# Two transformer layers on one core: query feature products moved to GpSimd, an elu without tanh, one more dense sequence, and a fixed priority table

## The chip, the cores and the metric

The kernel runs on one core of a Trainium2 chip, as one launch. Its time is device microseconds for the whole launch; a run's number is the median over executions. All tensors are float32.

## The reference, cut to what matters

The input is `x` of 8 sequences with 512 tokens of 128 features. Four blocks follow one another, each with a residual sum and a layer normalization.

```python
def feats(data, proj, is_query):               # random features, per head (16 heads of 64)
    dash = einsum('bnhd,md->bnhm', data * dn, proj)          # 64 features
    diag = sum(data**2, -1, keepdims=True) * dn*dn / 2
    mx = max(dash, -1) if is_query else max(dash)
    return ratio * (exp(dash - diag - mx) + 1e-6)

# block 1: linear attention, its own FFN and norms
qf, kf = feats(x@Wq, proj, True), feats(x@Wk, proj, False)
num = qf @ (kf^T v);  den = qf . sum_n(kf)                   # per head
out1 = layernorm(x + (num / den) @ Wo, g1, b1)
x = layernorm(x + layernorm(out1 + elu(out1@W1 + b1) @ W2 + b2, g2, b2'))
# block 2: mixture of 8 experts of width 64, top 2, every expert computed
x = layernorm(x + sum_e gates[e] * (gelu(x@w1[e] + b1[e]) @ w2[e] + b2[e]))
# block 3: softmax attention, 16 heads of 8, rotary
x = layernorm(x + softmax(rot(q) rot(k)^T / sqrt(8)) v @ wo + bo)
# block 4: mixture of 8 experts of width 176, top 2, and a shared expert
h = silu((x@w1[e] + b1[e]) * (x@w3[e] + b3[e]))
x = layernorm(x + sum_{2 chosen e} score[e] * (h@w2[e] + b2[e]) + shared(x))
```

## The kernel before, in words

**Stages.** `keys()` runs first, over all 8 sequences: key features, their exponentials, per sequence a 128 x 1024 product `xes`, and the sums of the key features over tokens, `z8` (8 x 1024, one row for each sequence, stored to `z_d`). It ends with a product `kvo` per sequence, stored to `kvo_d`. Then a loop runs over the sequences b. `linear_attention_and_ffn` (block 1) works in four tiles of 128 tokens. Its inner `features(t)` makes the query features: two projections into PSUM (L898, L908), Square on ScalarE (L903), sum (L905) and maximum (L914) per head, subtraction (L918), Exp (L919), the product with the row `zr` of key sums (L922), the sum of it per head (`den`, L924), its reciprocal (L926) and the scaling (L927). `attend(t)` transposes them (L937), copies (L941) and multiplies with `kvo` (L945). `features(t + 1)` is recorded ahead of `attend(t)`. The feed-forward has four chunks of 128 hidden units on 512 tokens (L970 to L979), with elu as Relu + min((Exp + 1) * Tanh, 0). `first_mixture` is block 2. `softmax_attention` (block 3) has 16 steps: four matmuls for 4 heads (L1147), Exp over 128 x 2048 in two activations (L1153), four matmuls with the values (L1159).

**Block 4 has two forms.** `GROUPS` lists the sequences that are sorted: `sort` scatters a sequence's tokens twice each with 8 indirect DMAs on GpSimd into `x_d` (L1469), by expert, and computes the shared expert (L1557, L1566). When a group is complete, `tiles` fetches weights and 256 tokens for each of a list of tiles, with `most = 2*N*n // TR + E2 - 1` entries for n sequences (L1620, L1626, L1634), and `combine` gathers the results of each sequence with 8 indirect DMAs (L1477) and sums them with the gates (L1653). A sequence in no group goes through `dense_mixture`: all experts and the shared one, as 13 chunks of 128 hidden units (L1328, L1329 the two projections, L1331 to L1339 the gating, L1353 the second product). Its weights `fw1`, `fw3`, `fw2` are loaded by `side_by_side`, after the linear attention of sequence 7 is recorded, and lie over the places of that stage.

**Places.** One SBUF tile `scratch` is cut by hand. On one side, from `feed_forward_at` on, lie the rings `f_zr`, `f_kvo`, `f_hT`, `f_res`, `f_o1`, `f_t0`, `f_t1`, then `a_xT`, `a_rot_q` and others. `fw1`, `fw3`, `fw2` (1664 elements each) and `m_gr` (5 x 512) lie from `feed_forward_at` on as well:

```python
fw1, fw3, fw2 = (scratch[:, feed_forward_at + FC2 * P * n :][:, 0 : FC2 * P] for n in range(3))
("m_gr", feed_forward_at + 3 * FC2 * P, 5), ("m_ta", KEYS_SCRATCH, 4), ("m_tb", KEYS_SCRATCH + 4 * N, 4),
```

**Order.** Every operation is first recorded in a `Schedule`, with an estimated time and with its dependences by place: two operations on overlapping places, one of which writes, keep the order in which they were recorded. `order()` then puts them in line: `latest_alone` gives each a latest start (from the due times, 40 us a sequence), and `forward` simulates all engines and takes next the operation that can start first, and among equals the one with the smaller latest start. It also chooses PSUM banks. Each operation belongs to a part, (stage, sequence): 0 linear attention, 1 first mixture, 2 softmax attention, 3 sort or dense mixture, 4 tiles, 5 combine, 6 `side_by_side`, and None. Before the change 400 rounds of random shifts of these parts follow, and the order with the shortest simulated span is issued. Each engine executes its own instructions in that order.

Of the kernel before, what the change touches and what calls it, by code (L numbers as in the profile page):

```python
# [30 lines left out]
F32 = mybir.dt.float32  # L31
AF = mybir.ActivationFunctionType
ALU = mybir.AluOpType
# [3 lines left out]
P = 128  # L37
# [14 lines left out]

GROUPS = ((0, 1, 2, 3), (4, 5, 6))

# [22 lines left out]
WAITS = mybir.DependencyInfo(mybir.DependencyClass.Sync, mybir.DependencyReason.DATA)  # L77
ROUNDS = 400
LATER = 8
PERIOD = 40.0  # L80


# [16 lines left out]
class Schedule:  # L99
# [171 lines left out]
    def order(self):  # L271

        self.tilings = [
            (self.tiling(w.calls[0]), self.tiling(w.calls[-1])) if w.engine == "PE" else None for w in self.works
        ]
        urgency = self.latest_alone()  # L280
        best = self.forward(urgency)
        again = self.backward(*best[:2])
        better = self.forward(again)
        if better is not None and better[0] < best[0]:
            best, urgency = better, again
        parts = sorted({w.part for w in self.works}, key=str)
        shift, chance = dict.fromkeys(parts, 0.0), random.Random(1)
        for _ in range(ROUNDS):
            trial = dict(shift)
            for _ in range(chance.choice((1, 1, 2, 3))):  # L290
                trial[chance.choice(parts)] += chance.gauss(0.0, chance.choice((3.0, 10.0, 30.0)))
            found = self.forward([u + trial[w.part] for u, w in zip(urgency, self.works)])
            if found is not None and found[0] <= best[0]:
                best, shift = found, trial
        self.makespan, self.starts, self.bank = best
        return [i for _, i in self.starts]

    def latest_alone(self):

        works, line, open_ = self.works, [], [len(w.before) for w in self.works]  # L300
        ready = [i for i, n in enumerate(open_) if not n]
        while ready:
            line.append(ready.pop())
            for j in works[line[-1]].after:
                open_[j] -= 1
                if not open_[j]:
                    ready.append(j)
        assert len(line) == len(works)
        latest = [0.0] * len(works)
        for i in reversed(line):  # L310
            w, end = works[i], self.ends[i]
            for j in w.after:
                end = min(end, latest[j] - self.HANDOVER[w.engine])
            latest[i] = end - max(w.us, w.lands)
        return latest

    def backward(self, span, starts):

        works, free = self.works, dict.fromkeys(self.HANDOVER, 0.0)
        key, latest, at = [0.0] * len(works), [0.0] * len(works), [0.0] * len(works)  # L320
        for start, i in starts:
            key[i] = -(start + works[i].us)
        open_, ready = [len(w.after) for w in works], {e: [] for e in free}
        for i, w in enumerate(works):
            if not w.after:
                bisect.insort(ready[w.engine], (key[i], i))
        for _ in works:
            best = None
            for e, waiting in ready.items():
                for entry in waiting:  # L330
                    end = max(free[e], at[entry[1]])
                    if best is None or end < best[0]:
                        best = (end, e, entry)
                    if end <= free[e]:
                        break
            end, e, entry = best
            ready[e].remove(entry)
            i = entry[1]
            free[e] = end + works[i].us
            done = end + max(works[i].us, works[i].lands)  # L340
            latest[i] = span - done
            for j in works[i].before:
                f = works[j].engine
                at[j] = max(at[j], done + (self.HANDOVER[f] if f != e else self.KEPT[f]))
                open_[j] -= 1
                if not open_[j]:
                    bisect.insort(ready[f], (key[j], j))
        return latest
# [121 lines left out]
def kernel(ctx: ExitStack, tc: tile.TileContext, i: dict, out: bass.AP):  # L470
# [104 lines left out]

    hb1 = keep("hb1", [P, FC])
    nc.vector.tensor_scalar(hb1, cols[:, C_B1 : C_B1 + FC], 0.5, None, ALU.mult)
    gb1 = keep("gb1", [P, 2])
# [5 lines left out]
    b1, fb = (rows[:, at : at + D] for at in (R_B1, R_FB2))  # L584
    nc.vector.tensor_tensor(b1, b1, fb, ALU.add)
    vv = keep("vv", [P, NT, V1])
    nc.gpsimd.memset(vv, 1.0)


    kvo_d = tc.dram_tile([B, P, 8, D], F32, name="kvo_d")  # L590
    z_d = tc.dram_tile([B, HM], F32, name="z_d")
    g1_d = tc.dram_tile([B, E1, N], F32, name="g1_d")
# [29 lines left out]
    def keys():  # L622
# [147 lines left out]
        )  # L770
        nc.sync.dma_start(z_d, z8)

# [39 lines left out]
    feed_forward_at = top["r"]  # L812
    ring("f_zr", 1, HM)
    ring("f_kvo", 1, 8, D)
    ring("f_hT", 1, FC, N)
    for name, n in (
        ("f_res", 2), ("f_o1", 1), ("f_t0", 2), ("f_t1", 2),
        ("a_xT", 1), ("a_rot_q", 1), ("a_rot_k", 1), ("a_t", 3), ("e_t", 2), ("a_o1", 1), ("a_res", 1), ("a_xa", 2),
        ("m_res", 1), ("m_xs", 1), ("m_ya", 2), ("m_t0", 1),
    ):  # L820
        ring(name, n, N)
# [64 lines left out]
    def linear_attention_and_ffn(b, xT):  # L886
# [7 lines left out]
        def features(t):  # L894
# [26 lines left out]
            pr = tile2("f_sp")  # L921
            nc.vector.scalar_tensor_tensor(pr, eq, EPS_KERN, zr, ALU.add, ALU.mult)  # L922
            den = tiny("f", [P, H], "den")
            nc.vector.tensor_reduce(den, hm(pr), AX.X, ALU.add)  # L924
            rden = tiny("f", [P, H], "rden")
            nc.vector.reciprocal(rden, den)  # L926
# [41 lines left out]
        for c in range(FC):  # L968
# [6 lines left out]
            nc.scalar.activation(ex, hp, AF.Exp, bias=bias)  # L975
            th = tile2("f_t1")
            nc.scalar.activation(th, hp, AF.Tanh, bias=hb1[:, c : c + 1], scale=0.5)
            nc.vector.scalar_tensor_tensor(ex, ex, 1.0, th, ALU.add, ALU.mult)
            nc.vector.scalar_tensor_tensor(hT[:, c, :], ex, 0.0, hT[:, c, :], ALU.min, ALU.add)  # L979
        fp = psb("fp", "f")  # L980
# [324 lines left out]
    def dense_mixture(xb, dst):  # L1305
# [15 lines left out]
        def hidden(c):  # L1321
# [15 lines left out]
            if gated:  # L1337
                nc.gpsimd.tensor_tensor(up, up, gr, ALU.mult)
            nc.vector.scalar_tensor_tensor(gr, ua, 1.0, up, ALU.add, ALU.mult)  # L1339
# [177 lines left out]
    def sort(b, xa, begin, group, rows_d):  # L1517
# [25 lines left out]
        for t in range(NT):  # L1543
            for k in range(2):
                nc.do(
                    "gpsimd", scatter(group), (rows_d,), (xa[:, t, :], slots[:, b, k, t : t + 1]),
                    1.05, 3.3, ("slots", group),
                )
# [95 lines left out]
    def combine(b, group, rows_d, dst):  # L1644
# [3 lines left out]
        for k in range(2):  # L1648
            y = tok(tile2("m_ya"))
            for t in range(NT):  # L1650
                nc.do("gpsimd", gather(group), (y[:, t, :],), (rows_d, slots[:, b, k, t : t + 1]), 1.05, 3.3)
            for t in range(NT):
# [155 lines left out]
```

## Time and profile before

| | |
|---|---|
| time, median of 3 runs | 1266.55 us (1265.4 to 1269.11) |
| the profiled execution: time, span | 1267.01 us, 1264.9 us |
| TensorE (PE) busy | 1152.9 us, 91% |
| VectorE (DVE) busy | 874.3 us, 69% |
| ScalarE (ACT) busy | 716.5 us, 57% |
| GpSimd (POOL) busy | 376.5 us, 30% |
| mean granted clock of TensorE | 0.954 |

Busy times overlap: the engines work side by side, and each waits for others by semaphores. A group's line reads: line of the kernel, engine, operation, destination <- sources, shape, count | busy us in all, mean ns of one | idle time of the engine just before them, and what ended it. `scratch` is the hand-cut tile, `ps` is PSUM. PEld is the weight load of TensorE. Matrix products in float32 take two passes, so each matmul of the code is two instructions in the profile. Sequences follow one another at some 115 us; the stages of neighbouring sequences overlap.

### The profile page before, as it was taken

How to read it: one execution, taken by the hardware profiler on the slowest of the kernel's cores; microseconds unless marked ns; L12 is line 12 of the kernel's file. 1: busy time of each engine (PE TensorE's matmuls, PEld its weight loads, DVE VectorE, ACT ScalarE, POOL GpSimd, SP SyncE). 2: the span in 40 equal slices, each digit the busy share in tenths (PEclk: the TensorE clock that was granted, in tenths of full speed). 3: DMA queues.
4: the chain of work that ended last, by engine and by line, in shares of the span. 5: the costliest groups of instructions: out<-in, count | busy, mean ns of one | idle time of the engine just before them, and what ended most of it. 6: DMA issues, size and time to landing. Idle time of an engine off the chain costs nothing. (4 is left out here: it accounts for less than half of the span.)

```text
span 1264.9 us, 17709 instructions
## 1 busy us (share of the span) xinstructions
PE 1152.9 (91%) x6262; PEld 626.0 (49%) x6262; DVE 874.3 (69%) x1940; ACT 716.5 (57%) x964; POOL 376.5 (30%) x375
## 2 busy tenths in 40 slices
PE   8999999978899999999899989999999885899972
PEld 4444445645543445535444546465456333654641
DVE  6766664988953964876885895678639477654763
ACT  3443444546377657576676555856664774277531
POOL 1242240022402400700720273122002877400174
PEclk9999999989999989999999989999999996899985
DMA  7038902301011002001101104223321224443241
GB/s 213 3 94 269 312 1 85 113 18 67 10 51 34 1 9 76 25 26 42 43 1 42 47 26 154 90 79 94 113 64 47 85 71 123 144 134 104 73 131 52
DMA packets 86747, 100.14 MB, mean 79 GB/s; under 512 B 17640, under 2 KB 62755, under 8 KB 86653
## 3 DMA queue, kind: packets, MB, share of 16 engines
q1 hardware_dynamic: 82765, 91.04, 23.6%
q0 software_dynamic: 3584, 7.35, 1.9%
q8 instruction: 51, 0.84, 0.3%
q10 hardware_dynamic: 304, 0.56, 0.1%
q14 instruction: 43, 0.35, 0.1%
HBM read 62.01 MB, written 39.93 MB: 81 GB/s over the span
## 5 line engine op out<-in xcount | busy, mean ns | idle before, releaser
L1153 ACT ACTIVATE scratch<-ps 128x1024 f32<-128x1024 f32 x256 | 248.9, 1022 | 103.8 <-PE ps L1147 102.8
L1147 PE MATMUL ps<-scratch 32*128 32x512 f32 x1024 | 163.4, 666 | 16.3 <-ACT scratch L1153 6.6
L1159 PE MATMUL ps<-scratch,vv 128*32 128x512 f32 x1024 | 140.7, 618 | 0.5 <-ACT scratch L1153 0.5
L853 POOL TENSOR_TENSOR f_ln_rs<-f_ln_ve,nhalf 128x4 f32<-128x4 f32 x24 | 27.5, 1146 | 212.1 <-DVE f_ln_ve L851 205.8
L664 ACT ACTIVATE scratch<-ps 128x1024 f32<-128x1024 f32 x32 | 32.7, 1023 | 92.4 <-PE ps L659 92.4
L1147 PEld LDWEIGHTS ps<-scratch 32*128 32x128 f32 x1024 | 45.7, 189 | 73.1 <-issue 22.4
L945 PEld LDWEIGHTS ps<-scratch 128*128 128x128 f32 x512 | 60.4, 192 | 19.1 <-issue 11.7
L1477 POOL DMA_INDIRECT scratch<-x_d,slots x56 | 56.3, 1005 | 41.6 <-DMA x_d<-scratch 24.0
L1626 PE MATMUL ps<-scratch 128*128 128x256 f32 x252 | 65.3, 398 | 1.6 <-DMA scratch<-w_d 0.8
L945 PE MATMUL ps<-scratch 128*128 128x128 f32 x512 | 64.0, 278 | 2.9 <-DVE a_ss L1013 1.0
L1123 POOL TENSOR_TENSOR scratch<-x_sb,rows 128x512 f32<-128x512 f32 x8 | 10.9, 1363 | 186.9 <-PE ps L613 184.5
L1469 POOL DMA_INDIRECT x_d<-scratch,slots x56 | 60.7, 1084 | 18.9 <-issue 14.7
L898 PE MATMUL ps<-wq,scratch 128*128 128x512 f32 x128 | 63.5, 603 | 0.8 <-DVE scratch L1094 0.8
L675 DVE SCALAR_TENSOR_TENSOR scratch<-k_ssq,ps 128x1024 f32<-128x1024 f32 x32 | 38.9, 1215 | 36.3 <-PE ps L669 32.4
L908 PE MATMUL ps<-wqf,scratch 128*128 128x512 f32 x128 | 63.4, 608 | 0.4 <-DVE scratch L1172 0.4
L1159 PEld LDWEIGHTS ps<-scratch,vv 128*32 128x32 f32 x1024 | 20.6, 109 | 82.0 <-issue 60.9
L659 PE MATMUL ps<-scratch 128*128 128x512 f32 x128 | 60.0, 608 | 0.7 <-ACT scratch L652 0.7
L698 PE MATMUL ps<-scratch,x_sb 128*128 128x512 f32 x128 | 59.4, 597 | 0.0
L669 PE MATMUL ps<-scratch 128*128 128x512 f32 x128 | 58.8, 598 | 0.0
L919 ACT ACTIVATE scratch<-scratch 128x1024 f32<-128x1024 f32 x32 | 33.9, 1058 | 43.1 <-DVE scratch L918 43.0
L1626 PEld LDWEIGHTS ps<-scratch 128*128 128x128 f32 x252 | 46.2, 195 | 20.1 <-issue 5.9
L941 ACT COPY scratch<-ps 128x1024 f32<-128x1024 f32 x32 | 32.3, 1010 | 34.3 <-PE ps L937 34.1
(281 smaller groups left out, 2528.7 us busy)
## 6 DMA issues: line engine op xcount, KB each, us to landing
x_d<-scratch SPq DMA_DIRECT2D x32, 512.0 KB, 8.5
scratch<-w_d SPq DMA_DIRECT2D x42, 386.0 KB, 3.1
scratch<-g_d SPq DMA_DIRECT2D x66, 128.0 KB, 3.1
scratch<-x_d SPq DMA_DIRECT2D x42, 128.0 KB, 2.1
x_d<-scratch SPq DMA_DIRECT2D x42, 128.0 KB, 1.9
kvo_d<-scratch SPq DMA_DIRECT2D x8, 512.0 KB, 5.7
scratch<-z_d SPq DMA_DIRECT2D x8, 512.0 KB, 4.4
scratch<-kvo_d SPq DMA_DIRECT2D x8, 512.0 KB
```

Source lines behind the costliest of these rows:

```text
L659: nc.tensor.matmul(kp_ps[:, a, :], xT[:, t * P : (t + 1) * P], wk[:, a * 512 : (a + 1) * 512], start=True, stop=True,)
L669: nc.tensor.matmul(dp_ps[:, a, :], xT[:, t * P : (t + 1) * P], wkf[:, a * 512 : (a + 1) * 512], start=True, stop=True,)
L698: nc.tensor.matmul(xp_ps[:, a, :], x_of(b)[:, t, :], ek[:, t, a * 512 : (a + 1) * 512], start=(t == 0), stop=(t == NT - 1),)
L898: nc.tensor.matmul(qp[:, a, :], xT[:, t * P : (t + 1) * P], wq[:, a * 512 : (a + 1) * 512], start=True, stop=True,)
L908: nc.tensor.matmul(dp[:, a, :], xT[:, t * P : (t + 1) * P], wqf[:, a * 512 : (a + 1) * 512], start=True, stop=True,)
L945: nc.tensor.matmul(at_ps[:, 0:D], qnT[:, c, :], kvo[:, c, :], start=(c == 0), stop=(c == 7))
L1147: nc.tensor.matmul(halves[g // 2][:, g % 2, :], kr[quarter, kt * P : (kt + 1) * P], qz[quarter, j, :], start=True, stop=True, tile_positio ...
L1153: nc.scalar.activation(pr[:, 2 * a : 2 * a + 2], sc, AF.Exp)
L1159: nc.tensor.matmul(av[32 * g : 32 * g + 32, :], vv[:, kt, head_columns(4 * g + j)], pr[:, g, :], start=(kt == 0), stop=(kt == NT - 1), til ...
L1469: inst = tc.nc.gpsimd.indirect_dma_start(out=rows_d, out_offset=bass.IndirectOffsetOnAxis(ap=slots_, axis=0), in_=tokens_, in_offset=None)
L1477: inst = tc.nc.gpsimd.indirect_dma_start(out=to, out_offset=None, in_=rows_d, in_offset=bass.IndirectOffsetOnAxis(ap=slots_, axis=0))
L1626: nc.tensor.matmul(to, w[:, c : c + P], xf, start=True, stop=True)
```

## The change

Four things are changed. (1) In `features`, the product of the query features with `zr` is a plain multiplication on GpSimd; the 1e-6 that was added to the features ahead of it becomes one number per head, made once per sequence in `keys()` (`z8e`), carried in 16 further columns of `z_d` and added to `den`. (2) elu is Relu + min(Exp, 1) - 1, and the -1 is taken out of the bias `b1` as the column sums of W2 (`less`); the Tanh, its bias `hb1`, one VectorE operation a chunk and the ring `f_t1` go. (3) `GROUPS` has sequences 0 to 3 and 4, 5; sequences 6 and 7 are both dense; the multiplication with the gates in the dense chunks goes from GpSimd to VectorE. (4) The planner starts from a fixed table of shifts by part and runs no rounds; the backward pass is gone, and its estimates for scatter and gather are 1.31 and 1.25 us instead of 1.05.

```diff
-GROUPS = ((0, 1, 2, 3), (4, 5, 6))
+GROUPS = ((0, 1, 2, 3), (4, 5))
...
-ROUNDS = 400
+ROUNDS = 0
+URGENT = {
+    (0, 0): 0.1, (0, 1): 12.6, (0, 2): -1, (0, 3): 35.5, (0, 4): 15.3, (0, 5): -2.6, (0, 6): 0.6,
...
+    (2, 4): -24.8, (2, 5): 25.4, (2, 6): -709.5, (2, 7): -55.9, (3, 0): 31.9, (3, 1): -290.8, (3, 2): 0.5,
+    (3, 3): -68.7, (3, 4): 183.1, (3, 5): 0.6, (3, 6): 81.4, (3, 7): 216.3, (4, 0): -18.1, (4, 1): 76.6,
+    (5, 0): 434, (5, 1): 631.3, (5, 2): 417.2, (5, 3): 926.4, (5, 4): 479.3, (5, 5): 341.1, (6, 0): -508.3,
+    None: 3.6,
+}
...
         urgency = self.latest_alone()
-        best = self.forward(urgency)
-        again = self.backward(*best[:2])
-        better = self.forward(again)
-        if better is not None and better[0] < best[0]:
-            best, urgency = better, again
...
+        shift, chance = {p: URGENT.get(p, 0.0) for p in parts}, random.Random(1)
+        best = self.forward([u + shift[w.part] for u, w in zip(urgency, self.works)])
...
+    less = nc.banks(1, 0)[:, 0, 0:D]
+    with nc.together():
+        for c in range(FC):
+            nc.tensor.matmul(less, ones, w2[:, c, :], start=(c == 0), stop=(c == FC - 1))
+    nc.vector.tensor_tensor(b1, b1, less, ALU.subtract)
...
-    z_d = tc.dram_tile([B, HM], F32, name="z_d")
+    z_d = tc.dram_tile([B, HM + H], F32, name="z_d")
...
-        nc.sync.dma_start(z_d, z8)
+        z8e = tiny("k", [B, H], "z8e", 1)
+        nc.vector.tensor_reduce(z8e, z8.rearrange("p (h m) -> p h m", m=M), AX.X, ALU.add)
+        nc.vector.tensor_scalar(z8e, z8e, EPS_KERN, None, ALU.mult)
+        nc.sync.dma_start(z_d[:, 0:HM], z8)
+        nc.sync.dma_start(z_d[:, HM:], z8e)
...
-    ring("f_zr", 1, HM)
+    ring("f_zr", 1, HM + H)
...
-        ("f_res", 2), ("f_o1", 1), ("f_t0", 2), ("f_t1", 2),
+        ("f_res", 2), ("f_o1", 1), ("f_t0", 2),
...
-            nc.vector.scalar_tensor_tensor(pr, eq, EPS_KERN, zr, ALU.add, ALU.mult)
+            nc.gpsimd.tensor_tensor(pr, eq, zr[:, 0:HM], ALU.mult)
             den = tiny("f", [P, H], "den")
             nc.vector.tensor_reduce(den, hm(pr), AX.X, ALU.add)
+            nc.vector.tensor_tensor(den, den, zr[:, HM:], ALU.add)
...
-            th = tile2("f_t1")
-            nc.scalar.activation(th, hp, AF.Tanh, bias=hb1[:, c : c + 1], scale=0.5)
-            nc.vector.scalar_tensor_tensor(ex, ex, 1.0, th, ALU.add, ALU.mult)
-            nc.vector.scalar_tensor_tensor(hT[:, c, :], ex, 0.0, hT[:, c, :], ALU.min, ALU.add)
+            nc.vector.scalar_tensor_tensor(hT[:, c, :], ex, 1.0, hT[:, c, :], ALU.min, ALU.add)
...
             if gated:
-                nc.gpsimd.tensor_tensor(up, up, gr, ALU.mult)
+                nc.vector.tensor_tensor(up, up, gr, ALU.mult)
...
                     "gpsimd", scatter(group), (rows_d,), (xa[:, t, :], slots[:, b, k, t : t + 1]),
-                    1.05, 3.3, ("slots", group),
+                    1.31, 3.6, ("slots", group),
...
-                nc.do("gpsimd", gather(group), (y[:, t, :],), (rows_d, slots[:, b, k, t : t + 1]), 1.05, 3.3)
+                nc.do("gpsimd", gather(group), (y[:, t, :],), (rows_d, slots[:, b, k, t : t + 1]), 1.25, 3.6)
```

## The prediction, made before the result was known

> **What bounds the kernel now.** The page's first table says TensorE, its windows say where not.
>
> ```profile
> PE 1152.9 (91%) x6262; PEld 626.0 (49%) x6262; DVE 874.3 (69%) x1940; ACT 716.5 (57%) x964; POOL 376.5 (30%) x375
> ```
>
> The span of 1264.9 us is 1152.9 of TensorE work and 112.0 of TensorE idleness, so a forecast is one for each of the two. The profiled execution took 1267.0 us, 2.1 outside its span; the median of the runs is 1266.55, so a span plus 1.7 stands for the median. Next the windows of 32 us: columns are the stretch, its length, busy time (and count) of PE, PEld, DVE, ACT and POOL, granted clock, DMA share, GB/s.
>
> ```profile
> 256.00:288.00 32.00, 22.41 (x95) 14.55 (x94) 27.46 (x61) 15.32 (x23) 7.85 (x6) 0.89 0.06 18
> 320.00:352.00 32.00, 28.10 (x139) 17.13 (x137) 31.43 (x73) 11.57 (x18) 13.27 (x12) 0.90 0.02 9
> 384.00:416.00 32.00, 31.14 (x192) 13.00 (x189) 13.39 (x32) 25.65 (x37) 7.59 (x7) 1.00 0.11 34
> 608.00:640.00 32.00, 28.28 (x142) 15.18 (x140) 29.58 (x47) 19.30 (x30) 22.11 (x24) 0.95 0.05 15
> 1056.00:1088.00 32.00, 16.95 (x70) 11.89 (x68) 18.68 (x82) 7.99 (x15) 20.62 (x34) 0.68 0.40 129
> 1216.00:1248.00 32.00, 21.32 (x103) 15.68 (x101) 16.89 (x42) 10.64 (x20) 23.76 (x23) 0.82 0.39 107
> ```
>
> TensorE idles where VectorE is nearly full (27 to 31 of 32 us) and hardly where VectorE is at 13. Adding up 32 minus the PE column over all windows: 6 us idle before 224, 18 in 224 to 352 (the first query features, nothing else to run yet), 36 in 352 to 1056, 15 in 1056 to 1088, 3 up to 1184, 34 from there to the end. The same windows have a granted clock of 0.68 to 0.95; busy time multiplied by one minus the clock gives some 24 us of stretched TensorE work in 224 to 1056, 5 in 1056 to 1088, 8 in the tail. The groups by line tell what fills VectorE there:
>
> ```profile
> L922 DVE SCALAR_TENSOR_TENSOR scratch<-scratch 128x1024 f32<-128x1024 f32 x32 | 38.9, 1216 | 7.5 <-ACT scratch L919 7.3
> L978 DVE SCALAR_TENSOR_TENSOR scratch<-scratch 128x512 f32<-128x512 f32 x32 | 22.9, 728 | 10.2 <-ACT scratch L977 10.1
> L977 ACT ACTIVATE scratch<-ps,hb 128x512 f32<-128x512 f32 x32 | 22.3, 697 | 0.0
> L708 POOL TENSOR_TENSOR scratch<-scratch 128x1024 f32<-128x1024 f32 x8 | 18.8, 2356 | 2.7 <-ACT scratch L693 2.7
> ```
>
> One token tile of query features costs VectorE L905, L914, L918, L922, L924, L927 at about 1.21 each and small ones, 8.2 us in all, against 7.1 of TensorE (L898, L908, L937, L945: 228.2 us over 32). Last the end: one line of TensorE's timeline, then the chain of waits (start, us, what):
>
> ```profile
> 1173.28 1.06 PE L1159 MATMUL ps<-scratch,vv 128*32 128x512 f32 x8
> ...
> 1195.11 1.05 POOL scratch L1477
> ...
> 1218.56 1.27 POOL scratch L1338
> ...
> 1248.97 1.07 POOL scratch L1477
> 1250.05 1.07 POOL m_ln_rs L853
> ```
>
> Attention of sequence 7 ends with these L1159, at 1174.3. The 91 us after it run on GpSimd: 24 gathers of the three sorted sequences, 1.25 apart, mixed with the 11 gate multiplications (L1338) of the dense sequence, whose L1353 matmuls wait for them (11.4 us in PEld's waits).
>
> **The change, part by part.** *Multiplication with the key sums to GpSimd.* VectorE loses 32 x 1.216 = 38.9 us and gains 32 small additions (den + zr's tail), 0.17 to 0.33 each by L916, the nearest 128x16 row: 5 to 10, I take 6. GpSimd gains 32 x 2.36 = 75.5 (L707 to L709, same shape); with 376 busy before it has room. The chain of one tile grows by 2.36 - 1.22 and one more handover (0.1 to 0.2 between neighbours in the timeline), 1.3 us; features(t+1) runs ahead of attend(t) and covers it; uncovered it is 32 x 1.3 = 42 us. VectorE's sum of a tile (L924) now waits for GpSimd, and L926, L927 and whatever VectorE has queued wait behind it. The long holders of GpSimd's queue there are the 8 scatters of a sorted sequence (1.27 to 1.39 us apart in the timeline), one instruction each, so one costs the multiplication at most 1.3 us of delay. z_d's second part costs one reduction and one tiny operation once, about 1.4 us of VectorE at 220, and one more DMA on SP: 1 us.
>
> *elu.* 32 Tanh activations (22.3 us of ScalarE) and 32 L978 (22.9 of VectorE) go; L979 stays in its form. The four `less` matmuls, once, in the setup: 0.5 us of TensorE.
>
> *Sequence 6 dense instead of sorted.* TensorE gains 13 chunks: 52 passes of 512 columns at 0.483 (L1557: 20.3/42) and 104 passes of 128 at 0.148 (L1566: 16.6/112), 25.1 + 15.4 = 40.5 (46.0 as the one dense sequence ran, at clock 0.82). It loses the shared expert (L1557, L1566: 2.9 + 2.4), the counting (0.8) and, since the list of group 1 shrinks from 19 tiles to 15, four tiles of 3.07 (L1620 16.8, L1626 65.3, L1634 46.8 over 42): 18.4. Net +22. GpSimd loses 8 scatters and 8 gathers (21 us with their gaps) and 11 L1338 (13.8), VectorE gains 22 multiplications of 0.74 (L1063's mean, 16.3) and about 20 of dense work, and loses 21 of sorting, tiles and combining. On SP four times two fetches and a store go, with sequence 6's store and load of xs_d; its gate rows and store of g2_d come.
>
> *The order.* All instructions are placed anew by a planner whose priorities are now a fixed table. Its worth has no row; I bound it by the idle time it can shift, the 36 + 15 + 3 us between 352 and 1184: none gained, or 30.
>
> **The sum, by stretches.** VectorE sheds 38.9 + 22.9 - 6 = 56 us, all in query features and feed-forward, where it is full. In 224 to 352 (8 tiles of 32, so 14 us) I let TensorE gain 10 of the 18 idle; in 352 to 1056 the other 42, cut by 10 for the lock below to 32, of which half, 18, reaches TensorE, because it idles in a part of these windows only. With less idle time I take a third of the stretched 24, 8 us, back. 1056 to 1088: the idle time came from sequence 6's routing ahead of tiles (L1526 waited 6.5 for L1522); dense work in its place leaves 8 of 15, and 3 of clock. Tail: attention output, normalization and router, 11.7 us from these operations' means and 0.1 a handover; 13 chunks at 2.9 with a fill of 4: 42; last sum and normalization 6.5; from there to the span's end 8.3, as now (1256.6 to 1264.9). Together 68.5 instead of 90.6, with 40 us of TensorE in it: 29 idle, 3 of clock won back. Idle: 7 + 8 + 18 + 8 + 5 + 29 = 75. Busy: 1152.9 + 22.5 - 8 - 3 - 3 = 1161.4. Span 1236.4, with 1.7 outside **1238**.
>
> **A rule against it.** GpSimd and VectorE get in each other's way in this trace:
>
> ```profile
> 521.98 1.26 POOL L1096 TENSOR_TENSOR scratch<-scratch 128x512 f32<-128x512 f32 x1
> 522.03 1.23 DVE L860 SCALAR_TENSOR_TENSOR a_ln_nm<-a_ln_mv,a_ln_rs 128x4 f32<-128x4 f32 x1 [1.58 <-POOL a_ln_rs L853]
> L916 DVE SCALAR_TENSOR_TENSOR f_nb<-f_ssq,f_mxq x32: 127/168/1239, 217.9 to 977.4; 128x16 f32<-128x16 f32 x32
> ```
>
> A VectorE operation of 0.16 us took 1.23 and ended with GpSimd's. L916 (minimum, median, maximum in ns) reaches 1239, L927 2108 over a median of 1215. Mean minus median, summed over L916, L927, L860, L979, L1285 and L1537, is some 21 us now. The multiplication adds 75.5 us of GpSimd beside 56 us of relief. By the rows' rate (21 us in 376 of GpSimd) it costs VectorE 4 us; if every one stops a VectorE operation for half its length, 32 x 1.18 = 38. I took 10. [...]
>
> **Rivals.** *All relief arrives* (0.23): idle time in 224 to 1056 falls from 54 to 14 and half the stretched 24 returns: 1238 - 12 - 4, and a few more in 1056 to 1184: **1219**. For it: VectorE is the only engine near full there. Against: the first features have nothing beside them, whichever engine is shorter.
>
> *The lock eats the relief* (0.08): 38 us of 56, and GpSimd's own waits the rest; 224 to 1056 keeps its idle time and clock, 1238 + 10 + 18 + 8 = **1274**. It decides once each multiplication meets one of its neighbours L916, den or L927. Against: they are three short turns of some 8 us.
>
> *Dense sequence 6 stands in attention 7's way* (0.13), the slower side: dropping f_t1 moves a_xT and a_rot_q down by 1008 elements; the dense part's ring m_gr (5 x 512 behind three 1664-wide weights, ending at 7552), now reaches past 6672 into both. Attention 7 cannot write its transposed input until the tenth chunk of sequence 6 is done. If nothing covers that, the front of dense 6 (11.7 + 4), the rest of its chunks' gaps (8) and attention 7's projections (8) stand open: 1238 + 32 = **1270**. It decides if group 1's 15 tiles (46 us of TensorE) and sequence 7's first mixture are used up before. For it: 1056 to 1088 now. Against: both become ready at that time.
>
> *The new order brings nothing* (0.04): table and costs fit no better, gains and the extra 22 us cancel: **1266**.
>
> **The numbers.** The forecast has 0.52, by itself 1226 to 1252. A measurement of this kernel tells about 0.3%, 4 us, from no change. Faster: 0.52 + 0.23 + 0.03 of the third rival: 0.78; same 0.05; slower 0.17. The range, 1214 to 1272, holds forecast, full relief and most of the third rival.
>
> **What would show it.** Right: L922 gone from DVE, a POOL line of 2.36 us x32, VectorE near 840 us, PE 1155 to 1175, windows with VectorE at 25 or less in query features and PE above 30 there, the end 65 to 72 us behind the last L1159 (90.6 now) without gathers in the chain. Wrong: PE idle 100 us or more; the chain waiting on GpSimd in query features; a stretch without L1147 while dense 6 runs with idle TensorE.

## The result, and the profile after

| | before | after |
|---|---|---|
| time, median of 4 runs each, taken side by side | 1265.97 us | 1225.57 us (1222.53 to 1226.43) |
| ratio, with its 95% interval | | 0.9673 [0.9648, 0.9699] |
| the profiled execution: time, span | 1267.01, 1264.9 us | 1222.53, 1220.7 us |
| TensorE idle, of the span | 112.0 us | 80.5 us |
| mean granted clock | 0.954 | 0.981 |
| time with the clock at half, added up from the trace's clock records | 119.6 us | 47.7 us |

The change makes the kernel 40 us faster; 28 were forecast. From the page after, the row of busy times and the row of granted clock in 40 slices; under them the clock row of the page before:

```profile
PE 1140.2 (93%) x6340; PEld 623.6 (51%) x6340; DVE 871.3 (71%) x1916; ACT 706.1 (58%) x943; POOL 417.5 (34%) x370
...
PEclk9999999989999999999999999999999999999988
```

```profile
PEclk9999999989999989999999989999999996899985
```

TensorE has 78 instructions more than before and is busy 12.7 us *less*. VectorE, which was to be relieved to some 840 us, is at 871, where it was. These two numbers are what the rest of this document is about. Four of the windows of 32 us that are shown of the kernel before (busy time and count of PE, PEld, DVE, ACT, POOL, then granted clock, DMA share, GB/s):

```profile
256.00:288.00 32.00, 27.11 (x121) 18.01 (x119) 23.16 (x49) 15.21 (x21) 14.27 (x8) 0.89 0.09 30
320.00:352.00 32.00, 27.99 (x151) 18.91 (x149) 28.87 (x66) 15.61 (x25) 19.83 (x14) 0.92 0.02 9
608.00:640.00 32.00, 29.88 (x146) 14.05 (x145) 31.56 (x45) 24.61 (x34) 21.62 (x14) 1.00 0.06 19
1056.00:1088.00 32.00, 29.90 (x180) 24.26 (x179) 25.20 (x54) 12.81 (x24) 1.01 (x1) 0.95 0.60 172
```

1056 to 1088 is filled: 29.9 of TensorE instead of 17.0. At 608 VectorE is as full as it was (31.6 us). The first query features (256, 320) still leave 4 to 5 us of each window idle, although 14 to 20 us of GpSimd now stand there. The groups of the changed lines, each shape by itself (busy, mean ns | idle time before and what ended it):

```profile
L912 POOL TENSOR_TENSOR scratch<-scratch 128x1024 f32<-128x1024 f32 x32 | 78.0, 2437 | 121.0 <-ACT scratch L909 74.7 <-ACT scratch L779 30.4 <-DVE f_den L914 12.5
L918 DVE SCALAR_TENSOR_TENSOR scratch<-scratch,f_rden 128x1024 f32<-128x1024 f32 x32 | 43.6, 1362 | 1.0
L914 DVE TENSOR_REDUCE f_den<-scratch 128x16 f32<-128x1024 f32 x32 | 38.6, 1205 | 11.3 <-POOL scratch L912 11.3
L967 DVE SCALAR_TENSOR_TENSOR scratch<-scratch 128x512 f32<-128x512 f32 x32 | 31.6, 999 | 4.8 <-ACT scratch L966 4.8
L915 DVE TENSOR_TENSOR f_den<-f_den,scratch 128x16 f32<-128x16 f32 x32 | 11.9, 372 | 0.2
```

L912 is the product on GpSimd, L914 the sum that waits for it, L915 the small addition, L967 the one operation left of elu's two on VectorE. L967 "stays in its form", as the prediction has it of L979, and its mean still went from 738 ns to 999; L979 before:

```profile
L979 DVE SCALAR_TENSOR_TENSOR scratch<-scratch 128x512 f32<-128x512 f32 x32 | 22.9, 738 | 2.9 <-ACT scratch L973 2.7
```

The tail, in TensorE's timeline (start, length, what, count, idle time before):

```profile
1150.11 2.98 PE L1147 MATMUL ps<-scratch,vv 128*32 128x512 f32 x16
...
1168.88 3.34 PE L1316 MATMUL ps<-scratch 128*128 128x512 f32 x4
...
1206.51 2.05 PE L1341 MATMUL ps<-scratch 128*128 128x128 f32 x16 [0.23 <-DVE scratch L1327]
```

Attention ends at 1153.1, the first dense chunk starts 15.8 us later, the 13 chunks take 39.7, and 12.1 more lead to the span's end at 1220.7: 67.6 us, with one gather, at their very start.

### The profile page after: what moved, and what is told of

Its sections match the earlier page's. It is cut to its first block, busy times and chain, and to the rows that moved or that the text cites. A ratio compares the mean times of both kernels' runs of the same rounds, so it can differ in the third digit from the quotient of the medians.

```text
span 1220.7 us, 17774 instructions
## 1 busy us (share of the span) xinstructions
PE 1140.2 (93%) x6340; PEld 623.6 (51%) x6340; DVE 871.3 (71%) x1916; ACT 706.1 (58%) x943; POOL 417.5 (34%) x370
## 5 line engine op out<-in xcount | busy, mean ns | idle before, releaser
L1135 PE MATMUL ps<-scratch 32*128 32x512 f32 x1024 | 152.9, 639 | 5.5 <-POOL scratch L1084 1.9
L1147 PE MATMUL ps<-scratch,vv 128*32 128x512 f32 x1024 | 138.1, 605 | 0.7 <-DVE scratch L939 0.5
L912 POOL TENSOR_TENSOR scratch<-scratch 128x1024 f32<-128x1024 f32 x32 | 78.0, 2437 | 121.0 <-ACT scratch L909 74.7
L936 PEld LDWEIGHTS ps<-scratch 128*128 128x128 f32 x512 | 60.3, 192 | 19.3 <-issue 9.4
L1465 POOL DMA_INDIRECT scratch<-x_d,slots x48 | 48.0, 999 | 49.8 <-issue 41.3
L1614 PE MATMUL ps<-scratch 128*128 128x256 f32 x228 | 55.7, 383 | 0.8 <-DVE scratch L1610 0.7
L1457 POOL DMA_INDIRECT x_d<-scratch,slots x48 | 47.5, 990 | 23.3 <-issue 9.5
L651 DVE TENSOR_REDUCE k_ssq<-scratch 128x16 f32<-128x1024 f32 x32 | 38.8, 1216 | 17.1 <-ACT scratch L649 17.1
L692 POOL TENSOR_TENSOR scratch<-scratch 128x1024 f32<-128x1024 f32 x7 | 16.5, 2364 | 97.4 <-PE ps L654 64.5
```

The lines of the kernel that those rows point to most:

```text
L912: nc.gpsimd.tensor_tensor(pr, eq, zr[:, 0:HM], ALU.mult)
L936: nc.tensor.matmul(at_ps[:, 0:D], qnT[:, c, :], kvo[:, c, :], start=(c == 0), stop=(c == 7))
L1135: nc.tensor.matmul(halves[g // 2][:, g % 2, :], kr[quarter, kt * P : (kt + 1) * P], qz[quarter, j, :], start=True, stop=True, tile_positio ...
L1147: nc.tensor.matmul(av[32 * g : 32 * g + 32, :], vv[:, kt, head_columns(4 * g + j)], pr[:, g, :], start=(kt == 0), stop=(kt == NT - 1), til ...
L1465: inst = tc.nc.gpsimd.indirect_dma_start(out=to, out_offset=None, in_=rows_d, in_offset=bass.IndirectOffsetOnAxis(ap=slots_, axis=0))
L1614: nc.tensor.matmul(to, w[:, c : c + P], xf, start=True, stop=True)
```

## The experiments

Two theories stood against each other. RELIEF: the changed operations make TensorE wait less (the prediction's sum). ORDER: most of the gain is the new order of instructions. The runs fall into three sets; each set ran on one chip, with the kernel before beside it, and chips differ (the kernel before took 1264.8, 1277.9 and 1272.7 us on them). So ratios are compared, and kernels within a set.

### First set: order and operations apart

**No table.** The changed kernel with all shifts at zero.

```diff
-URGENT = { ... }
+URGENT = {}
```

> The changed kernel with an empty table of shifts and no rounds: the planner's first order as it falls out. Theory ORDER (the table carries most of the 40 us, the moved operations little): 1255 to 1270. Theory RELIEF (VectorE's relief and the shorter end carry it, the table little): 1230 to 1240.

Measured: 1275.4 us, ratio 1.0093 [1.0068, 1.0118]. Without its table the changed kernel is 0.9% slower than the kernel before, more than either theory had.

**The planner of before, the new operations.** `order()` and `backward` of before, 400 rounds.

```diff
-ROUNDS = 0
+ROUNDS = 400
...
-        best = self.forward([u + shift[w.part] for u, w in zip(urgency, self.works)])
+        best = self.forward(urgency)
+        again = self.backward(*best[:2])
+        better = self.forward(again)
...
```

> All operations of the changed kernel, with the planner of the kernel before (backward pass and its 400 rounds). Theory ORDER: 1250 to 1265, near the kernel before. Theory RELIEF: 1228 to 1238.

Measured: 1260.04 us, ratio 0.9960 [0.9944, 0.9975]. All the changed operations together, ordered as the kernel before was, bring 5 us.

**The operations of before, a searched table.** Nothing but the order, with the PSUM banks that the planner picks along with it, is changed; the shifts come from 20,000 rounds of the changed planner's search, written into the kernel.

```diff
-ROUNDS = 400
+ROUNDS = 0
+URGENT = { ... }   # 20,000 rounds, from zero
...
```

> All operations of the kernel before, with the changed planner and a table of shifts found for them by 20000 rounds of the changed kernel's search. Theory ORDER: 1235 to 1248, most of the way to the changed kernel with none of its operations. Theory RELIEF: 1258 to 1268.

Measured: 1233.12 us, ratio 0.9747 [0.9723, 0.9771]. No operation is changed and 32 us are gone. Its page:

```profile
PE 1133.3 (92%) x6262; PEld 619.0 (50%) x6262; DVE 872.4 (71%) x1940; ACT 716.1 (58%) x964; POOL 379.8 (31%) x375
...
PEclk9999999999999999999998999999999899899977
```

The same 6262 matmul instructions as before are busy 19.6 us less, and TensorE's idle time fell by 14.8. VectorE has what it had (872.4, before 874.3).

**Another table for the changed kernel,** from the same search started at zero.

```diff
-URGENT = { (0, 0): 0.1, ... }
+URGENT = { ... }   # 20,000 rounds, from zero
```

> The changed kernel with another table, found by 20000 rounds from zero: shows how much two tables of the same kind differ on the chip and is the mate of the searched kernels to come. Theory ORDER: 1215 to 1230. Theory RELIEF: within 6 us of 1225.6 as well.

Measured: 1230.15 us (1224.6 to 1237.5), ratio 0.9746 [0.9706, 0.9786]: 45 us below the same operations without a table. The four medians of this chip make a square: 1264.8 before, 1233.1 with the order alone, 1260.0 with the operations alone, 1230.2 with both. The order is worth 30 to 32 us of it, the operations 3 to 5; the two kernels with searched tables have ratios that can't be told apart (0.9747 and 0.9746). ORDER holds for this square. Each corner is one table, however, and two tables of the changed kernel lie at 0.9673 and 0.9746 on two chips, so 3 to 5 us for the operations is no more than two tables can differ by.

### Second set: one part undone, each with a table of its own

Each kernel takes one part back and gets its own table from 20,000 rounds, so that a part isn't judged in an order made for another.

```diff
# product_on_vector
-            nc.gpsimd.tensor_tensor(pr, eq, zr[:, 0:HM], ALU.mult)
+            nc.vector.tensor_tensor(pr, eq, zr[:, 0:HM], ALU.mult)
# elu_with_tanh
+            th = tile2("f_t1")
+            nc.scalar.activation(th, hp, AF.Tanh, bias=hb1[:, c : c + 1], scale=0.5)
+            nc.vector.scalar_tensor_tensor(ex, ex, 1.0, th, ALU.add, ALU.mult)
-            nc.vector.scalar_tensor_tensor(hT[:, c, :], ex, 1.0, hT[:, c, :], ALU.min, ALU.add)
+            nc.vector.scalar_tensor_tensor(hT[:, c, :], ex, 0.0, hT[:, c, :], ALU.min, ALU.add)
...            # less goes; f_t1 and hb1 as before
# three_sorted_one_dense
-GROUPS = ((0, 1, 2, 3), (4, 5))
+GROUPS = ((0, 1, 2, 3), (4, 5, 6))
# rings_apart: f_t1 keeps its place, unused
-        ("f_res", 2), ("f_o1", 1), ("f_t0", 2),
+        ("f_res", 2), ("f_o1", 1), ("f_t0", 2), ("f_t1", 2),
```

Product back on VectorE:

> The changed kernel with the query features' product on VectorE again (all else as changed), with a table of its own from 20000 rounds. To be read beside the changed kernel with its own searched table, 1230.2, and the recorded table, 1225.6. Theory RELIEF (half of 38.9 us of VectorE reaches the end, as forecast): 1242 to 1250. Theory ORDER (with a good order VectorE is not what TensorE waits for): 1225 to 1238.

elu with the Tanh:

> The changed kernel with the Tanh form of elu again (32 Tanh activations, 32 more VectorE operations, the ring f_t1 back in its place), table of its own from 20000 rounds. Theory RELIEF (half of 22.9 us): 1235 to 1243. Theory ORDER: 1224 to 1235.

Sequence 6 sorted again:

> The changed kernel with sequence 6 sorted again (groups of 4 and 3, one dense), table of its own from 20000 rounds. The forecast's terms: 16 to 22 us less TensorE work, an end that is 22 to 28 us longer (gathers behind the last attention). If both terms hold: 1228 to 1240. If the dense sequence is a loss once the order is good: 1210 to 1222.

The places of attention 7 moved out of the dense ring's reach (the slower rival's mechanism):

> The changed kernel with the unused ring f_t1 left in its place, so that m_gr again lies over no a_xT and a_rot_q, table of its own from 20000 rounds. Third rival (the places hold attention 7 back): 8 us or more below 1225 to 1230, with a shorter way from the last linear attention to attention 7. Else within 5 us of them.

| | us | ratio, interval |
|---|---|---|
| product_on_vector | 1256.35 | 0.9842 [0.9786, 0.9898] |
| elu_with_tanh | 1257.16 | 0.9829 [0.9775, 0.9882] |
| three_sorted_one_dense | 1245.34 | 0.9758 [0.9703, 0.9814] |
| rings_apart | 1247.01 | 0.9761 [0.9710, 0.9813] |

The intervals are wide because the kernel before scattered on this chip (1271.8 to 1285.6), and the changed kernel itself has no run here; its nearest stand-in is rings_apart, which has all its operations. Set beside the runs of rings_apart (1244.0 to 1248.7), those with the product on VectorE (1255.1 to 1261.4) and with the Tanh (1254.1 to 1259.5) don't overlap and are some 10 us slower; those with sequence 6 sorted (1244.0 to 1250.8) are the same. Each kernel has one table, and two tables can differ by as much, so a price for a single part doesn't follow. Two things can be read: every kernel with a searched table is faster than before, whichever part it lacks, and neither the second dense sequence nor moving the rings apart shows a gain. The expectations were in microseconds of the first chip and can't be held against this one.

### Third set: one part undone in the same order

Here the changed kernel's order and its PSUM banks are written out as a list, so that taking a part back moves nothing else.

**The control**, the changed kernel from that list:

```diff
-        best = self.forward([u + shift[w.part] for u, w in zip(urgency, self.works)])
...
-        return [i for _, i in self.starts]
...
+        self.bank = dict(enumerate(PINNED_BANK))   # the banks, as a list
+        return list(ORDER)                         # the order, as a list
```

> The changed kernel with its order and PSUM banks written out as a list instead of being planned: the same instructions in the same order, as the mate of the three pinned kernels in this call. Both theories: 0.967 of the kernel before, as the changed kernel.

Measured: 1253.32 us (1250.1 to 1261.6), ratio 0.9843 [0.9826, 0.9859]. Every engine has the instructions that gave 1225.57 us and 0.9673 on the result's chip. This was not expected; the last section returns to it. The control's trace is of its slowest run (1261.6 us), so the rows below show it somewhat longer than its median.

**The product on VectorE, in this order** (the diff of product_on_vector):

> The changed kernel's order, unchanged, with the 32 products of the query features on VectorE instead of GpSimd: 32 x 1.22 = 39 us more on VectorE, 78 less on GpSimd, no other difference and no other table. Theory RELIEF: 15 to 30 us slower than the control, the time lost in the windows of query features. Theory ORDER: within 6 us of the control, since what the table gained does not depend on VectorE's load.

Measured: 1244.16 us, ratio 0.9778 [0.9763, 0.9792], 9 us *faster* than the control, which neither theory had.

**A small product.** Only the first 16 of the 1024 columns are multiplied, in place; the rest of the product is left out. The handovers from Exp to the product and from the product to the sum stay; the second place `f_sp` isn't written any more, so waits for it go too.

```diff
-            nc.gpsimd.tensor_tensor(pr, eq, zr[:, 0:HM], ALU.mult)
+            nc.gpsimd.tensor_tensor(eq[:, 0:H], eq[:, 0:H], zr[:, 0:H], ALU.mult)
-            nc.vector.tensor_reduce(den, hm(pr), AX.X, ALU.add)
+            nc.vector.tensor_reduce(den, hm(eq), AX.X, ALU.add)
```

> The changed kernel's order with the product on GpSimd cut to 16 of its 1024 columns (in place, so den leaves out the key sums for the rest): VectorE waits for a GpSimd operation of about 0.15 us instead of 2.44, and GpSimd is out of VectorE's way for 73 us. If length and lock of the product cost time: 8 to 20 us faster than the control, with L914's wait of 11.3 us gone and L915 and L918 near 0.17 and 1.22. If they are covered: within 4 us.

Measured: 1227.78 us, ratio 0.9637 [0.9604, 0.9670], 25.5 us faster than the control, more than the 8 to 20 expected. L914's wait for the product falls from 11.3 us to 2.8; the product itself still takes 308 ns (2451 in the control), about twice what was expected.

**elu with the Tanh, in this order:** the Tanh right behind the Exp, its VectorE operation right ahead of the one that stays.

```diff
-            nc.scalar.activation(ex, hp, AF.Exp, bias=bias)
-            nc.vector.scalar_tensor_tensor(hT[:, c, :], ex, 1.0, hT[:, c, :], ALU.min, ALU.add)
+            th = tile2("f_t1")
+            with nc.together():
+                nc.scalar.activation(ex, hp, AF.Exp, bias=bias)
+                nc.scalar.activation(th, hp, AF.Tanh, bias=hb1[:, c : c + 1], scale=0.5)
+            with nc.together():
+                nc.vector.scalar_tensor_tensor(ex, ex, 1.0, th, ALU.add, ALU.mult)
+                nc.vector.scalar_tensor_tensor(hT[:, c, :], ex, 0.0, hT[:, c, :], ALU.min, ALU.add)
...
```

> The changed kernel's order with the Tanh form of elu put back in place: 22.3 us more of ScalarE and 22.9 of VectorE, behind the Exp and ahead of the last operation of each chunk (less is then multiplied by 0). Theory RELIEF: 10 to 20 us slower than the control. Theory ORDER: within 6 us.

Measured: 1277.89 us, ratio 1.0059 [1.0037, 1.0082], 24.6 us slower than the control: here RELIEF (10 to 20) was nearer than ORDER (within 6). The busy rows of the four pages, the control first, then product on VectorE, small product and Tanh:

```profile
PE 1164.5 (92%) x6340; PEld 633.0 (50%) x6340; DVE 866.1 (69%) x1916; ACT 706.0 (56%) x943; POOL 416.7 (33%) x370
```

```profile
PE 1153.8 (93%) x6340; PEld 625.7 (50%) x6340; DVE 871.9 (70%) x1948; ACT 706.2 (57%) x943; POOL 342.4 (28%) x338
```

```profile
PE 1150.5 (94%) x6340; PEld 624.8 (51%) x6340; DVE 832.6 (68%) x1916; ACT 706.1 (57%) x943; POOL 346.9 (28%) x370
```

```profile
PE 1164.6 (91%) x6340; PEld 632.1 (50%) x6340; DVE 896.1 (70%) x1949; ACT 723.5 (57%) x975; POOL 417.6 (33%) x370
```

Look at the DVE column. The product on VectorE costs 42.0 us there (32 operations of 1312 ns), yet VectorE's total rises by only 5.8. The lengths of the *other* VectorE operations sum to 32 us less than in the control (the rest of the difference is overlap, which the total counts once). One of these rows, the small addition, in the control (L1181 there is L915) and with the product on VectorE:

```profile
L1181 DVE TENSOR_TENSOR f_den<-f_den,scratch 128x16 f32<-128x16 f32 x32 | 11.9, 372 | 0.2
```

```profile
L1181 DVE TENSOR_TENSOR f_den<-f_den,scratch 128x16 f32<-128x16 f32 x32 | 7.9, 248 | 0.2
```

The Tanh shows the opposite: 30.0 us more of VectorE and 17.5 of ScalarE, nothing given back, and 24.6 us of time.

## Why the prediction was right or wrong

The number, the sign and the range were right, and the reasons for them largely not: the forecast's 28 us came from relief of VectorE and the shorter tail, the measured 40 mostly from the order. That the time fell near the forecast is in good part luck. Idle time came out at 80.5 us against 75 because its errors cancel: 13 and 9 us too much in 224 to 352 and 352 to 1056, 16 too little behind. Of the five signs that were to show it right, L912 on GpSimd and the tail came; VectorE near 840, PE from 1155 to 1175 and the windows of query features did not.

**Dense sequence 6 and the tail: the length right, the credit not.** L1316, L1317 and L1341 take 28.1, 26.5 and 26.8 us for two sequences, 40.7 each (40.5 foreseen). The tail is 67.6 us (68.5): its front longer than foreseen (15.8 against 11.7), its chunks shorter (39.7 against 42 with their fill). Every other kernel of the first set with two dense sequences has 66 to 67 us there, whatever its order, and the searched table with one dense has 95.7. So the gain of 23 us at the end belongs to part (3) of the change, but not to dense sequence 6 alone: the two kernels above 90 us also have the multiplication with the gates on GpSimd, between the gathers. In the searched one that multiplication (L1354) stands behind nine gathers in GpSimd's queue, and TensorE waits for VectorE's operation behind it (L1355):

```profile
1178.67 2.07 PE L1369 MATMUL ps<-scratch 128*128 128x128 f32 x8 [8.09 <-DVE scratch L1355]
```

`three_sorted_one_dense` has sequence 6 sorted and this multiplication on VectorE. All its 24 gathers stand behind its last attention product (first and last):

```profile
1166.57 1.07 PE L1147 MATMUL ps<-scratch,vv 128*32 128x512 f32 x8
...
1172.12 1.05 POOL L1465 DMA_INDIRECT scratch<-x_d,slots  x1 [22.61 <-DMA x_d<-scratch]
...
1222.78 3.36 POOL L1465 DMA_INDIRECT scratch<-x_d,slots  x1 [0.30 <-issue]
```

From 1167.6 to the span's end at 1242.2 it takes 74.6 us. So some 16 of the 23 us come without a second dense sequence, and only about 7 with it. That the place of the multiplication makes the difference, and not this kernel's table, no run shows by itself. Against them stands the additional TensorE work of the next paragraph, and the second set doesn't show a price for sorting sequence 6 again.

**TensorE's work: mis-sized.** Busy was to be 1161.4 and is 1140.2, the largest miss of the sum. It has two halves. Busy time multiplied by the clock, over the windows of 32 us, is some 1114 us before and 1124 after: about 10 more, where net 22.5 were counted. It is 16 more with the planner of before and 17 more in the control, which has the instructions of after, so the estimate is good to some 7 us. The stretched part, busy time multiplied by one minus the clock, went from 38.7 to 16.2 us: 22.5 came back, where the terms for the clock were 8, 3 and 3.

**Relief of VectorE: the step that failed.** The sum gave 10 us of idle time in 224 to 352 and 18 in 352 to 1056 to a VectorE shorter by 56 (the second from half of 32, which is 16: a slip of 2). Measured: 21.1 us idle in the first (18.1 before), 27.2 in the second (36.1; the control, with the same instructions, has 38.5). The path of one tile got longer, too: L914 waits 11.3 us for L912, TensorE's transposes 7.1 for the scaled features (4.5 before). With the small product 224 to 352 has 14.4 us idle, 20.7 in the control and 19.5 with the product on VectorE: what the first query features gain by a VectorE without the product they lose by GpSimd's length and by the waiting beside it, which these runs don't separate. And VectorE was not relieved, because the term that the prediction calls the lock, taken at 10 us, was too small. No run shows a lock as such, or these 10 us; what the runs show in their place is VectorE operations that start beside a product and end only after it. Adding up what each of VectorE's operations took above the median of its line: 53 us before, 79 after. The same sum in one order is 72 with the product on GpSimd (control), 45 with the product on VectorE and 39 with the small product. So a product costs VectorE (72 - 45) / 32, some 0.85 us, a good third of its length; 27 us in all, and well above the 10 that the value leaned to. The summed lengths of the third set say 32, and so do the meetings themselves. In the changed kernel 53 VectorE operations start beside one of the 32 products (L912) and would, at their median, end before it. 21 of them are held until it has ended, 31.6 us over their medians: all 19 with two inputs from SBUF, and two tensor_scalar operations. The other 32, which are reductions, batch norms, reciprocals and operations with an input from PSUM, keep their length within 0.04 us. This lies near the upper of the prediction's two ends (4 and 38). One such meeting, both engines, and L1021's line as it was before (L1033 there):

```profile
363.81 2.38 POOL L912 TENSOR_TENSOR scratch<-scratch 128x1024 f32<-128x1024 f32 x1 [3.35 <-ACT scratch L909]
364.03 2.44 DVE L1021 TENSOR_TENSOR scratch<-a_lg 128x256 f32<-128x256 f32 x1
```

```profile
L1033 DVE TENSOR_TENSOR scratch<-a_lg 128x256 f32<-128x256 f32 x8 | 3.3, 416 | 0.0
```

It took 0.42 in the mean before; here it starts 0.2 after the product and ends 0.3 after it. The prediction showed a row of this kind (1.23 us for an operation of 0.16) and then priced the effect nearer to the rate of a sparser queue, 4 us, than to its own other end, 38.

**The rivals.** "The lock eats the relief" had the right effect and the wrong place in the account: the relief of the product is eaten (5.8 us of VectorE's busy time left of 42), and the kernel is faster all the same. It was named as a slower outcome since nothing else was thought to carry a gain. "All relief arrives" was nearest to the time, 1219, by a fall of idle time from 54 to 14 that did not happen (48 are left). "Dense sequence 6 stands in attention 7's way" did not show: 2 us idle in 1056 to 1088, where 8 were left by the forecast; the run that moves the rings apart has no mate on its chip and decides nothing. "The new order brings nothing" is refuted, with a sign: the order was the largest term.

**The order: the missing term.** It was bounded as "none gained, or 30" of idle time, and none entered the sum under its own name. With no operation changed it is worth 32 us, and more than half of that is not idle time at all: over the profiled executions, 34.4 us apart, the operations of before in the searched order have 14.8 us less TensorE idle, 14.8 less stretched by the clock and about 5 less that neither explains. A bound by idle time alone left that part out.

**elu: right in kind, small in the sum.** In the changed kernel's order its undoing costs 24.6 us, with TensorE 110 us idle instead of the control's 95 (span minus PE). That order was made for the shorter elu. In the second set, with a table of its own, the kernel with the Tanh is some 10 us slower than rings_apart.

**The product on GpSimd: not shown to help.** In the changed kernel's own order it costs 9 us, on the one chip where that was run. With tables of their own, in the second set, the kernel without it is some 9 us slower than rings_apart. The two disagree in sign, and 9 us is less than the changed kernel moved from one chip to the other; what the product on GpSimd would bring in the best order for each is open.

## What to carry to other kernels

Price an order of instructions like an operation, and try the new order with the old operations before crediting the operations: here it was most of the gain. In these runs half clock followed 24 of the 47 pieces of 3.41 us in which TensorE was 40 to 50% busy, and all 122 in which it was less: an idle gap near 2 us is to be priced with the half clock that may follow it, so a wait removed can pay twice (with the order alone, 14.8 us of idle time and 14.8 of stretched work), and one added as well. Of 42.0 us of products given to GpSimd only 5.8 left VectorE's total, and all 19 operations with two inputs from SBUF that would have ended beside a product were held until it had ended: undo such a move in a fixed order and compare VectorE's total, not the group's.

## What the runs showed of the hardware

**How short a gap stood ahead of half the clock.** The trace's clock records know two values, 1 and 0.5, in pieces of 3.41 us (before and after, every record of half clock lasts 3.41 us or a multiple of it, up to 20.48, but for the last of each trace). Each of the 14 profiled executions is laid here on its own grid of such pieces, as its clock records have it; for pieces at full clock from 205 us on, the table has TensorE's busy share and whether the next piece was at half clock:

| busy share of the piece | pieces | followed by half clock |
|---|---|---|
| under 0.4 | 122 | 122 |
| 0.4 to 0.5 | 47 | 24 |
| 0.5 to 0.6 | 87 | 19 |
| 0.6 to 0.7 | 102 | 16 |
| 0.7 and more | 3605 | 6 |

So in these executions all 122 pieces that were more than 60% idle, 2 us and more, were followed by at least 3.41 us at half the clock, 24 of the 47 that were 40 to 50% busy, and 6 of the 3605 that were busy for 70% and more. Idle time in the midst of a busy stretch therefore counts by how it falls on the grid: a gap of 2.45 us within one piece, busy otherwise, leaves it 0.28 busy, in the row with 122 of 122; split evenly over two, it leaves each 0.64 busy, in the row with 16 of 102.

**The same instructions, 1225 and 1253 us.** The changed kernel on the result's chip and its control in the third set (their profiled executions took 1222.5 and 1261.6 us) keep within 1.1 us of each other up to 527 us. Then both have the same gap (TensorE's timeline, after and control):

```profile
527.96 1.24 PE L1554 MATMUL ps<-sw,scratch 128*128 128x128 f32 x9 [2.45 <-DVE scratch L1503]
```

```profile
527.06 2.26 PE L1820 MATMUL ps<-sw,scratch 128*128 128x128 f32 x9 [2.46 <-DVE scratch L1769]
```

The windows around it, each execution on its own grid, after first (the last number before DMA share and GB/s is the clock):

```profile
523.10:526.50 3.40, 2.41 (x14) 1.20 (x12) 3.33 (x5) 3.40 (x5) 2.88 (x3) 1.00 0.00 0
526.50:530.00 3.50, 2.04 (x20) 1.95 (x24) 3.50 (x6) 1.24 (x2) 0.57 (x1) 1.00 0.00 0
530.00:533.40 3.40, 3.05 (x24) 0.54 (x24) 3.40 (x3) 1.25 (x2) 1.81 (x2) 1.00 0.00 0
536.80:555.00 18.20, 18.20 (x128) 8.70 (x120) 10.29 (x40) 13.18 (x16) 12.43 (x22) 1.00 0.12 37
```

```profile
522.40:525.80 3.40, 2.20 (x13) 1.01 (x11) 3.37 (x5) 3.40 (x6) 2.68 (x2) 1.00 0.00 0
525.80:529.20 3.40, 2.14 (x10) 2.17 (x11) 3.40 (x5) 1.02 (x2) 0.67 (x1) 0.51 0.00 0
529.20:532.70 3.50, 3.50 (x20) 1.61 (x19) 3.50 (x5) 0.00 (x0) 1.71 (x2) 0.51 0.00 0
536.10:555.00 18.90, 17.77 (x113) 8.12 (x112) 7.25 (x27) 11.18 (x15) 12.85 (x22) 1.00 0.11 36
```

Both have the gap split over two windows that are 0.58 to 0.71 busy. One keeps the clock, the other loses it for two windows, comes later with its matmuls, and idles 1.1 us more behind it. At 566 us of the changed kernel the control is 8.9 us behind, at 749 14.4, at 953 25.1. At each step stands a half-clock piece that the other execution doesn't have (525.8, 556.6, 727.2, 751.1 and 925.2 us); the changed kernel ran 618 us without one. The clock is not all of it: some 4 us of the first step come at full clock, between 549 and 557 us, with gaps of TensorE for which the trace shows no wait. Of the 39 us between the two spans 17 are stretched TensorE work, 15 idle time and 7 neither. The two are also the fastest of the changed kernel's runs and the slowest of the control's.

**What stays open.** Where the grid falls differs from execution to execution (counted from the span's start, a piece begins every 3.41 us from 0.7 us on in the kernel before, from 0.9 in the changed kernel and from 0.2 in the control), but that alone doesn't explain the distance: all 5 runs of the control lie above all 4 of the changed kernel on the result's chip, and the kernel before was 0.5% slower there too (1272.7 against 1266.0). What differs between the chips isn't shown by these traces. So the 40 us are measured on the result's chip, the same instructions bring 19 on the other, and of the shares named here those within one set stand firmest.
